# One product for each block of z and its convolution, in a two-layer graph network on one Trainium2 core

## The chip, the cores and the metric

The kernel runs on one core of one Trainium2 chip. It is one launch that computes the whole network. The metric is the device time of one execution in microseconds (us); the times given are medians of several executions. A core has five engines, each with its own in-order queue of instructions: TensorE (PE), which multiplies matrices into PSUM; VectorE (DVE); ScalarE (ACT); GpSimd (POOL); and SyncE (SP), which here only issues transfers. An instruction that waits holds everything behind it in its queue.

## What is computed

The network has 3125 nodes of 256 channels, 50,000 edges and two layers. Each layer adds to x a graph block and a mixing block, and then a feed-forward block. The change concerns the mixing block of the second layer, a hyperbolic linear attention. Cut to what matters (the sequence length is 1, so of each width-5 convolution only the centre tap acts, and `proj`, `expmap0` and `logmap0` reduce to scalings of a row by a function of its norm):

```python
h = conv1d(logmap0(proj(x, c), c), w_qkv, pad=2)       # 256 -> 768 channels
h = relu(batchnorm(h, bn_gamma, bn_beta))
t = logmap0(proj(proj(expmap0(h, c), c), c), c)
s = conv1d(t, w_dw, pad=2, groups=t.shape[1])          # one weight per channel
s = conv1d(s, w_pw, pad=0, groups=t.shape[1] // DIM)   # 24 blocks of 32 x 32
cat = concatenate([t, s], axis=1)                      # 1536 channels
t2 = logmap0(proj(proj(expmap0(cat, c), c), c), c)
q, k, v = split(t2.reshape(N, 16, 96, L), 3, axis=2)   # 16 heads of 32
vk = einsum('ngdl,ngel->ngde', v, relu(k))
out = einsum('ngde,ngdl->ngdl', vk, relu(q)) / (sum(v, -1) + ATT_EPS)
```

After it come another norm, a 512 to 256 convolution `w_res` with its bias, and a last hyperbolic scaling.

## The kernel before

The nodes lie in 25 tiles of 125 rows; four tiles form a chunk (the last chunk is one tile). The first layer, and the product that makes the 768 channels `z` of the second, run until about 1234 us. `z` is stored in DRAM in transposed form: channels on partitions, nodes in the free dimension.

Then `layer1` plans its work. Streams are written as Python generators that yield `Op(engine, cost, ...)` before each step. `Flow.run` is a planner: it picks, again and again, the step that can start earliest by the costs in the code (ties go by urgency), and the order in which the steps are picked is the order of the instructions on all engines. A step can take and give buffers by name: `z` has one buffer, `cat`, `r`, `ST` and `Sb` two, `S` and `kvg` three, and `nm` is a set of three PSUM banks that many streams share. The costs decide the order; at run time each engine follows that order and waits where a result is late.

The streams of this stage are:

- `group` and `attend`, the edge attention, 25 blocks (`b`) of 17 slots in three groups. POOL gathers rows of k and v (line 1524, `kvg`). SP loads the queries `q3` (line 1532), the one-hot matrices `ST` (line 1537) and `Sb` (line 1545). ACT widens `Sb` to `S` (line 1551). PE spreads the queries (line 1560, `qe`), DVE multiplies by k (line 1564), sums per head (line 1583, `sco`), ACT takes the exponential (line 1590), DVE weights v (line 1593), and PE sums over the edges (line 1601, `es`). `attend` then divides and multiplies by a weight matrix (`wvT` line 1619, `wp` line 1626).
- `hyper`, the mixing block, one stream per tile, two tiles sharing one `z` load (a pair, 13 in all). It is the code that changes.
- `hyper_end`, its last norms per chunk, and `mlp_stream`, the graph block's feed-forward part (`hp_g` line 703, `dn_g` line 717).
- After all edge blocks: routing, the scatter of rows (line 1980) and the expert products (lines 2083 and 2098), with the shared expert (`hp_s` line 2009, `dn_s` line 2023) beside them on PE until the end.

In `hyper`, the pair's `z` comes by one transfer on SP (line 1642) and ACT applies batch norm and relu to its six blocks of 128 channels (line 1645). The channels are arranged so that block `3 * h + m` holds four heads' groups of one kind: `m` is 0 for k, 1 for q, 2 for v, and `h` is the half. Four PSUM accumulators `cat_{t}_{i}` follow for each tile. Accumulators 0 and 1 hold three blocks each, transposed by PE (line 1662); 2 and 3 hold the convolution of three blocks each (line 1664), where `bd` holds the six 128 x 128 block-diagonal matrices of `w_pw`, scaled by `w_dw` (line 1484). ACT empties each: the first two by one copy (line 1674), the others by a relu of k (line 1676) and a copy of q and v (line 1677), and each by a square whose row sums go to `n2` (line 1679). The last product of a pair's second tile frees `z`, and the next pair's load may then start. DVE and ACT form the attention from `cat` (lines 1685 to 1715), PE transposes it (line 1720) and multiplies by `wres` (line 1727).

The tile `wxt`, which `bd` views, serves the first layer before: its columns hold the weights `wx` of the products `xm` (line 921), which end at about 88 us. Then `w_pw` is loaded into it (line 1474).

Of the kernel before, what the change touches and what calls it, by code (L numbers as in the profile page):

```python
# [7 lines left out]
F32 = mybir.dt.float32  # L8
BF16 = mybir.dt.bfloat16
I32 = mybir.dt.int32  # L10
AF = mybir.ActivationFunctionType
OP = mybir.AluOpType
AX = mybir.AxisListType
# [7 lines left out]
P = 125  # L21
# [10 lines left out]
NH, HD = 8, 32  # L32
# [118 lines left out]
def kernel(ctx: ExitStack, tc: tile.TileContext, a: dict, out: bass.AP):  # L151
    nc = tc.nc


    keep = ctx.enter_context(tc.tile_pool(name="keep", bufs=1))
# [16 lines left out]
    def nm_tile(shape, name):  # L172
        return ps_tile("nm", shape, name)
# [59 lines left out]

    wxt = keep.tile([128, 6 * 128], F32, name="wxt")
    xbt = keep.tile([128, C + 1 + 2 * NH * 4], F32, name="xbt")
# [14 lines left out]
    ident = keep.tile([128, 128], F32, name="ident")  # L250
# [19 lines left out]
    tiny = keep.tile([128, 1], F32, name="tiny")  # L270
# [128 lines left out]
    for k in range(2):  # L399
        po = nm_tile([128, 2 * NQ], f"wxqk_{k}")  # L400
# [1062 lines left out]
    def layer1(lists):  # L1463
# [8 lines left out]
        wp = lp.tile([128, 2, C], F32, name="wp")  # L1472
        bd = wxt.rearrange("p (m d) -> p m d", m=6)
        nc.sync.dma_start(out=bd, in_=a["w_pw"].rearrange("m p d -> p m d"))
# [157 lines left out]
        def hyper(t, pair, ch):  # L1632
# [18 lines left out]
            todo = []  # L1651
            for i in range(4):
                s, h = divmod(i, 2)
                last = i == 3 and t == t0 + nt - 1
                mk = yield Op("PE", 0.48 if s == 0 else 0.86, [pair["ready"]],
                              take=["nm"] + (["cat"] if i == 0 else []),
                              give=["z"] if last else [])
                po = nm_tile([P, 3, 128], f"cat_{t}_{i}")
                for m in range(3):
                    zm = pair["z"][:, 3 * h + m, at_]  # L1660
                    if s == 0:
                        nc.tensor.transpose(po[:, m, :], zm, ident)
                    else:
                        nc.tensor.matmul(po[:, m, :], zm, bd[:, 3 * h + m, :],
                                         start=True, stop=True)
                todo.append((mk, po, i))
                while len(todo) == 2 or (todo and i == 3):
                    mk, po, q = todo.pop(0)
                    full = yield Op("ACT", 1.15 if q < 2 else 1.35, [mk],
                                    give=["nm"])  # L1670
                    if q == 0:
                        cat = lp.tile([P, 4, 3, 128], F32, tag="cat", name=f"cat_{t}", bufs=2)
                    if q < 2:
                        nc.scalar.copy(cat[:, q], po)
                    else:
                        nc.scalar.activation(cat[:, q, 0, :], po[:, 0, :], AF.Relu)
                        nc.scalar.copy(cat[:, q, 1:, :], po[:, 1:, :])
                    sq = lp.tile([P, 512], BF16, tag="sq", name=f"sq_{t}_{q}")
                    nc.scalar.activation(sq[:, :384], po.rearrange("p m d -> p (m d)"), AF.Square,
                                         accum_out=pair["n2"][:, t - t0, q : q + 1])  # L1680
# [3 lines left out]
            m = yield Op("DVE", 0.68, [full])  # L1684
            nc.vector.tensor_reduce(ks, cat[:, :, 0, :].rearrange("p q (g d) -> p q g d", d=HD),
                                    AX.X, OP.add)
            s12 = ch["s12"][:, j : j + 1]
            if t == t0 + nt - 1:
                m = yield Op("DVE", 0.4, [m, full])
                nn = lp.tile([P, 2], F32, tag="nn", name=f"nn_{t}", bufs=2)[:, :nt]  # L1690
                nc.vector.tensor_reduce(nn, pair["n2"][:, :nt, :], AX.X, OP.add)
                nc.vector.tensor_scalar(nn, nn, MIN_NORM ** 2, None, op0=OP.max)
                y, m = yield from rsqrt_by_power(nn, nt, f"nn{t}", m)
                m = yield Op("DVE", 0.17, [m])
                nc.vector.tensor_scalar(ch["s12"][:, j + 1 - nt : j + 1], y, ATANH_MAXN, 1.0,
                                        op0=OP.mult, op1=OP.min)
                pair["scale"].set(m)
# [3 lines left out]
            r = lp.tile([P, 4, 128], F32, tag="r", name=f"r_{t}", bufs=2)  # L1701
            nc.scalar.activation(r, cat[:, :, 2, :], AF.Identity, bias=tiny[:P], scale=s12)
            for q in range(2):
                m = yield Op("DVE", 1.7, [m])
                nc.vector.reciprocal(r[:, 2 * q : 2 * q + 2, :], r[:, 2 * q : 2 * q + 2, :])  # L1705
            m = yield Op("DVE", 0.68, [m])
            nc.vector.scalar_tensor_tensor(r, cat[:, :, 2, :], s12, r, op0=OP.mult, op1=OP.mult)
            m = yield Op("DVE", 0.68, [m], give=["cat"])
            nc.vector.scalar_tensor_tensor(r, cat[:, :, 1, :], 0.0, r, op0=OP.max, op1=OP.mult)
            m = yield Op("DVE", 0.68, [m])  # L1710
# [15 lines left out]
            for k in range(4):  # L1726
                nc.tensor.matmul(po, oT[:, k, :], wres[:, k, :], start=(k == 0), stop=(k == 3))  # L1727
            m = yield Op("ACT", 0.4, [m, ms], take=["ft"], give=["nm"])
# [614 lines left out]
```

## Time and profile before

| | us |
|---|---|
| median of 5 runs | 2729.35 |
| lowest, highest | 2724.88, 2730.55 |
| the profiled execution | 2732.3 |
| its span in the profile | 2730.4 |
| PE busy over the span | 2496.3 (91%) |
| DVE busy | 1338.2 (49%) |
| ACT busy | 983.6 (36%) |
| POOL busy | 1189.2 (44%) |
| mean granted PE clock | 0.961 |

The instructions of `hyper` that change, in the stage from 1234 to 2072 us, count and mean duration:

| line, engine | what | count | mean ns |
|---|---|---|---|
| 1662 PE | transposes, 128 columns | 150 | 288 |
| 1664 PE | convolution products, 128 columns (two records each) | 300 | 285 |
| 1674 ACT | copy of 384 | 50 | 478 |
| 1676 ACT | relu of 128 | 50 | 288 |
| 1677 ACT | copy of 256 | 50 | 388 |
| 1679 ACT | square of 384 | 100 | 516 |
| 1679 ACT | reading its row sums | 100 | 224 |

How to read the profile: it is one execution taken by the hardware profiler. Busy time is the union of the recorded durations of an engine. The recorded end of a PE instruction is modelled, and neighbouring records of PE and of ACT overlap, so the pace of a run of instructions is read from their starts. A product of two fp32 operands leaves two records, a transpose one. "A <- B" in the waits means that an instruction of A stood idle until B was done. The chain that ended last is followed back from the last instruction, at each step to what released it or to the instruction before it on its engine; in this profile it reaches back to 1522 us. Lines are those of the kernel before.

### The profile page before, as it was taken

To read this page: it belongs to the slowest core of one execution; us is meant where nothing else is said; L and a number is where in the kernel's file an instruction comes from. 1 tells how busy PE (TensorE), PEld (TensorE's weight loads), DVE (VectorE), ACT (ScalarE), POOL (GpSimd) and SP (SyncE) were. 2 spreads that over 40 slices of the span, in tenths; PEclk is the share of its full clock that TensorE was granted. 3 is DMA by queue.
4 is the path that set the end of the run, shared out by engine and by line. 5 is a ranking of instruction groups with operands and counts; after the bars stand their busy time and mean duration, and the time that the engine had idled before them with its cause. 6 is when DMAs were issued, how large, how long until landed. Compare 5 with 4: busy or idle time off the path is not lost. (4 is left out here: it accounts for less than half of the span.)

```text
span 2730.4 us, 32036 instructions
## 1 busy us (share of the span) xinstructions
PE 2496.3 (91%) x11409; PEld 1825.1 (67%) x11409; DVE 1338.2 (49%) x3226; ACT 983.6 (36%) x2013; POOL 1189.2 (44%) x1179
## 2 busy tenths in 40 slices
PE   5888989999999999986779888998989999999998
PEld 4555666666666555565656666767767678888886
DVE  7365123353624344266888788888885201111113
ACT  4772112222323343344336444464432222222221
POOL 3002777777770000005775676656622722222220
PEclk9989999999999999997889999999999999999999
DMA  4425666576761015127776667666620245555555
GB/s 119 161 82 178 169 196 185 167 219 176 208 186 32 1 49 148 48 64 234 235 215 186 183 209 212 187 198 195 200 76 1 79 158 192 192 203 187 195 181 149
DMA packets 186996, 426.99 MB, mean 156 GB/s; under 512 B 31433, under 2 KB 116553, under 8 KB 178634
## 3 DMA queue, kind: packets, MB, share of 16 engines
q0 software_dynamic: 80688, 281.78, 34.3%
q1 hardware_dynamic: 103593, 140.99, 16.5%
q10 hardware_dynamic: 2545, 2.09, 0.3%
q8 instruction: 92, 1.51, 0.2%
q14 instruction: 78, 0.64, 0.1%
HBM read 358.95 MB, written 65.74 MB: 156 GB/s over the span
## 5 line engine op out<-in xcount | busy, mean ns | idle before, releaser
L1524 POOL DMA_INDIRECT kvg<-kvtab,el x425 | 466.0, 1096 | 232.3 <-issue 109.1
L1083 POOL DMA_INDIRECT msg<-hs,el x425 | 418.5, 985 | 322.7 <-DMA hot<-S 193.4
L1195 ACT ACTIVATE fh<-fp,bnh,bns 128x500 f32<-128x500 f32 (+1 forms) x224 | 160.7, 723 | 371.8 <-PE fp L1191 371.5
L1601 PE MATMUL es<-kvg,S 128*125 128x264 f32 x850 | 225.7, 419 | 40.9 <-DVE kvg L1593 40.4
L2071 ACT ACTIVATE rhid<-rh,rw 128x256 f32<-128x256 f32 x256 | 121.3, 474 | 342.0 <-PE rh L2083 341.3
L2083 PE MATMUL rh<-xrT,rw 128*128 128x256 f32 x1024 | 238.3, 381 | 0.0
L1206 DVE SCALAR_TENSOR_TENSOR x<-fy,f_w,x 125x256 f32<-125x256 f32 x200 | 96.2, 482 | 276.2 <-PE fy L1203 275.8
L2098 PE MATMUL ry<-rw,rhid 128*128 128x256 f32 x1024 | 231.5, 379 | 0.0
L1601 PEld LDWEIGHTS es<-kvg,S 128*125 128x125 f32 x850 | 169.7, 204 | 88.6 <-DVE kvg L1593 52.9
L1112 PEld LDWEIGHTS <-S 128*125 128x125 bf16 x1275 | 153.0, 138 | 103.1 <-issue 85.6
L1560 PE MATMUL qe<-q,ST 125*128 125x256 bf16 x1275 | 179.3, 284 | 43.7 <-DVE kvg L1564 38.4
L1112 PE MATMUL es<-msg,S 128*125 128x256 bf16 x1275 | 182.0, 276 | 34.3 <-DMA msg<-hs,el 27.4
L2098 PEld LDWEIGHTS ry<-rw,rhid 128*128 128x128 f32 x1024 | 194.6, 190 | 26.5
L2083 PEld LDWEIGHTS rh<-xrT,rw 128*128 128x128 f32 x1024 | 193.2, 191 | 25.7 <-issue 0.5
L1203 PE MATMUL fy<-f_Wo,fh 128*125 128x256 f32 x800 | 205.5, 380 | 1.2 <-DVE x L1206 0.8
L2105 DVE TENSOR_TENSOR yr<-ry,rw 128x256 f32<-128x256 f32 x64 | 27.2, 425 | 359.7 <-PE ry L2098 359.7
L1191 PE MATMUL fp<-fh,f_W 128*128 128x500 f32 (+1 forms) x448 | 186.4, 545 | 0.3 <-ACT fh L1195 0.3
L1191 PE MATMUL fp<-xT_f,f_W 128*128 128x500 f32 (+1 forms) x448 | 186.5, 544 | 0.0
L1560 PEld LDWEIGHTS <-ST 125*128 125x128 bf16 x1275 | 128.7, 101 | 85.1 <-issue 54.4
L1319 POOL TENSOR_TENSOR xn<-xn,row_bp 125x1024 f32<-125x1024 f32 (+1 forms) x7 | 13.8, 1977 | 389.1 <-DVE hx L1293 319.1
L1203 PEld LDWEIGHTS fy<-f_Wo,fh 128*125 128x125 f32 x800 | 142.1, 188 | 54.6 <-issue 33.3
L1564 DVE TENSOR_TENSOR kvg<-qe,kvg 128x512 f32<-128x512 f32 (+1 forms) x225 | 144.8, 651 | 44.1 <-DMA kvg<-kvtab,el 26.2
(425 smaller groups left out, 4214.5 us busy)
## 6 DMA issues: line engine op xcount, KB each, us to landing
db<-dlT SPq DMA_DIRECT2D x25, 544.0 KB
ST<-dlT SPq DMA_DIRECT2D x25, 544.0 KB
hot<-S SPq DMA_DIRECT2D x50, 187.5 KB
Sb<-hot SPq DMA_DIRECT2D x50, 187.5 KB
ztab<-z SPq DMA_DIRECT2D x18, 500.0 KB
z<-ztab SPq DMA_DIRECT2D x12, 750.0 KB
xs<-pad SPq DMA_DIRECT2D x1, 8224.0 KB
xr<-xs SPq DMA_DIRECT2D x32, 257.0 KB
```

The lines of the kernel that those rows point to most:

```text
L1083: nc.gpsimd.indirect_dma_start(out=msg[:, i, :], out_offset=None, in_=hs3_rows, in_offset=bass.IndirectOffsetOnAxis(ap=el[:, b, g0 + i : g ...
L1112: nc.tensor.matmul(blk["po"], S[:, i, :], msg[:, i, r * C : (r + 1) * C], start=(g0 + i == 0 and r == 0), stop=(g0 + i == LE - 1 and r == 2))
L1191: nc.tensor.matmul(ps[q][:, :n], self.ws[e][i][:, k, q * 128 : (q + 1) * 128], h[:, k, :n], start=(k == 0), stop=(k == 1))
L1195: nc.scalar.activation(nxt[:, q, :n], ps[q][:, :n], AF.Relu, bias=self.sh[i][:, 2 * e + q : 2 * e + q + 1], scale=self.sc[i][:, 2 * e + q ...
L1203: nc.tensor.matmul(po, nxt[:, k, j * P : (j + 1) * P], self.ws[e][2][:, k, :], start=(k == 0), stop=(k == 1))
L1524: nc.gpsimd.indirect_dma_start(out=kvg[:, i, : 2 * C], out_offset=None, in_=kvtab, in_offset=bass.IndirectOffsetOnAxis(ap=el[:, b, g0 + i ...
L1560: nc.tensor.matmul(pq[i0][:, i, :], ST[:P, g0 + i0 + i, :], blk["q3"][:, r, :], start=(r == 0), stop=(r == 2))
L1564: nc.vector.tensor_tensor(kvg[:, i0 : i0 + k, :C], pq[i0][:, :k, :], kvg[:, i0 : i0 + k, :C], OP.mult)
L1601: nc.tensor.matmul(blk["pa"], S[:, i, :], kvg[:, i, C:], start=(g0 + i == 0), stop=(g0 + i == LE - 1))
L2071: nc.scalar.activation(hid[-1][:, q % 2, :], ps, AF.Gelu, bias=w1[:, 8 * C + q : 8 * C + q + 1])
L2083: nc.tensor.matmul(ps, w1[:, k * 4 * C + h * 128 : k * 4 * C + (h + 1) * 128], xrT[:, k, :], start=(k == 0), stop=(k == 1))
L2098: nc.tensor.matmul(po, hid[k // 2][:, k % 2, r * 128 : (r + 1) * 128], w2[:, k * C : (k + 1) * C], start=(k == 0), stop=(k == 7))
```

## The change

`wxt` grows from six blocks of 128 columns to seven. Block 0 is filled with the identity by DVE at the beginning of `layer1`; the six convolution matrices follow it as blocks 1 to 6. A block of `z` is then multiplied once, with a right-hand side of 256 columns that takes block 0 and block `3 * h + i + 1` with a step between them, so that one product gives the transposed block and its convolution side by side. The transposes are gone.

A tile has three accumulators in place of four, one for each kind: k, q and v. Each is 512 columns: block and convolution of half 0, block and convolution of half 1. ACT empties the accumulator of k by one relu of 512 and those of q and v by one copy of 512, and each by one square of 512. `cat` is arranged by kind accordingly, so that DVE and ACT read contiguous columns later; the four sums of squares become three; and the rows of `wres` are taken in another order, since the order of the 512 attention channels is now half, then block before convolution. The planner's costs of these steps change with them: four PE steps of 0.48, 0.48, 0.86 and 0.86 us become three of 0.95, and four ACT steps of 1.15, 1.15, 1.35 and 1.35 become three of 1.4.

```diff
-    wxt = keep.tile([128, 6 * 128], F32, name="wxt")
+    wxt = keep.tile([128, 7 * 128], F32, name="wxt")
...
-        bd = wxt.rearrange("p (m d) -> p m d", m=6)
+
+        both = wxt.rearrange("p (m d) -> p m d", m=7)
+        nc.vector.tensor_copy(both[:, 0, :], ident)
+        bd = both[:, 1:, :]
         nc.sync.dma_start(out=bd, in_=a["w_pw"].rearrange("m p d -> p m d"))
...
-            for i in range(4):
-                s, h = divmod(i, 2)
-                last = i == 3 and t == t0 + nt - 1
-                mk = yield Op("PE", 0.48 if s == 0 else 0.86, [pair["ready"]],
+            for i in range(3):
+                last = i == 2 and t == t0 + nt - 1
+                mk = yield Op("PE", 0.95, [pair["ready"]],
                               take=["nm"] + (["cat"] if i == 0 else []),
                               give=["z"] if last else [])
-                po = nm_tile([P, 3, 128], f"cat_{t}_{i}")
-                for m in range(3):
-                    zm = pair["z"][:, 3 * h + m, at_]
-                    if s == 0:
-                        nc.tensor.transpose(po[:, m, :], zm, ident)
+                po = nm_tile([P, 4, 128], f"cat_{t}_{i}")
+                for h in range(2):
+                    nc.tensor.matmul(po[:, 2 * h : 2 * h + 2, :], pair["z"][:, 3 * h + i, at_],
+                                     both[:, 0 : 3 * h + i + 2 : 3 * h + i + 1, :], start=True, stop=True)
+                todo.append((mk, po, i))
+                while len(todo) == 2 or (todo and i == 2):
+                    mk, po, q = todo.pop(0)
+                    full = yield Op("ACT", 1.4, [mk], give=["nm"])
+                    if q == 0:
+                        cat = lp.tile([P, 3, 4, 128], F32, tag="cat", name=f"cat_{t}", bufs=2)
+                        nc.scalar.activation(cat[:, 0], po, AF.Relu)
                     else:
-                        nc.tensor.matmul(po[:, m, :], zm, bd[:, 3 * h + m, :],
-                                         start=True, stop=True)
-                todo.append((mk, po, i))
-                while len(todo) == 2 or (todo and i == 3):
-                    mk, po, q = todo.pop(0)
-                    full = yield Op("ACT", 1.15 if q < 2 else 1.35, [mk],
-                                    give=["nm"])
-                    if q == 0:
-                        cat = lp.tile([P, 4, 3, 128], F32, tag="cat", name=f"cat_{t}", bufs=2)
-                    if q < 2:
                         nc.scalar.copy(cat[:, q], po)
-                    else:
-                        nc.scalar.activation(cat[:, q, 0, :], po[:, 0, :], AF.Relu)
-                        nc.scalar.copy(cat[:, q, 1:, :], po[:, 1:, :])
                     sq = lp.tile([P, 512], BF16, tag="sq", name=f"sq_{t}_{q}")
-                    nc.scalar.activation(sq[:, :384], po.rearrange("p m d -> p (m d)"), AF.Square,
+                    nc.scalar.activation(sq, po.rearrange("p q d -> p (q d)"), AF.Square,
                                          accum_out=pair["n2"][:, t - t0, q : q + 1])
...
-            nc.vector.tensor_reduce(ks, cat[:, :, 0, :].rearrange("p q (g d) -> p q g d", d=HD),
+            nc.vector.tensor_reduce(ks, cat[:, 0].rearrange("p q (g d) -> p (q g) d", d=HD),
...
-                nc.vector.tensor_reduce(nn, pair["n2"][:, :nt, :], AX.X, OP.add)
+                nc.vector.tensor_reduce(nn, pair["n2"][:, :nt, :3], AX.X, OP.add)
...
-            nc.scalar.activation(r, cat[:, :, 2, :], AF.Identity, bias=tiny[:P], scale=s12)
+            nc.scalar.activation(r, cat[:, 2], AF.Identity, bias=tiny[:P], scale=s12)
...
-            nc.vector.scalar_tensor_tensor(r, cat[:, :, 2, :], s12, r, op0=OP.mult, op1=OP.mult)
+            nc.vector.scalar_tensor_tensor(r, cat[:, 2], s12, r, op0=OP.mult, op1=OP.mult)
...
-            nc.vector.scalar_tensor_tensor(r, cat[:, :, 1, :], 0.0, r, op0=OP.max, op1=OP.mult)
+            nc.vector.scalar_tensor_tensor(r, cat[:, 1], 0.0, r, op0=OP.max, op1=OP.mult)
...
-                nc.tensor.matmul(po, oT[:, k, :], wres[:, k, :], start=(k == 0), stop=(k == 3))
+                nc.tensor.matmul(po, oT[:, k, :], wres[:, 2 * (k % 2) + k // 2, :], start=(k == 0), stop=(k == 3))
```

## The prediction

> **What bounds the kernel now.** I read four views: busy time by stretch, the waits, the chain that ended last, and the timelines of TensorE (PE) and ScalarE (ACT) around the products that change.
>
> The changed products run only in the second layer's planned stage, from 1234 to about 2072 us. Busy time by stretch; the columns are stretch, length, then busy us (and instructions) of PE, PE weight loads, VectorE (DVE), ACT and GpSimd (POOL), granted PE clock, DMA share, GB/s:
>
> ```profile
> 1234.00:1521.00 287.00, 222.27 (x1182) 173.68 (x1182) 227.19 (x382) 130.02 (x330) 186.12 (x173) 0.88 0.73 224
> 1521.00:2014.00 493.00, 436.16 (x2321) 338.43 (x2321) 413.90 (x680) 238.47 (x552) 303.44 (x278) 0.95 0.62 189
> 2014.00:2072.00 58.00, 50.78 (x220) 38.77 (x218) 51.27 (x198) 19.22 (x45) 12.17 (x9) 0.91 0.07 21
> 2072.00:2215.00 143.00, 136.55 (x543) 92.65 (x542) 35.94 (x111) 33.01 (x52) 73.92 (x108) 0.98 0.27 83
> 2215.00:2730.00 515.00, 508.23 (x2383) 439.38 (x2381) 76.07 (x183) 131.17 (x275) 122.13 (x124) 0.99 0.54 181
> ```
>
> To see: over the stage's 838 us PE is busy 709 us (85%), DVE 692 (83%), ACT 388 (46%). No engine is saturated; PE and DVE share the bound through waits on each other. After 2072 us PE is busy 136.55 + 508.23 of 658 us, so whatever the stage gains or loses arrives at the end undiminished. The waits of the stage say the same (engine, line, what released it: us in total, times, longest):
>
> ```profile
> PE es L1601 <- DVE kvg L1593: 40.4, 29, 6.2
> PE qe L1560 <- DVE kvg L1564: 38.4, 30, 4.8
> DVE kvg L1564 <- DMA kvg<-kvtab,el: 26.2, 11, 9.1
> DVE kvg L1593 <- ACT kvg L1590: 15.8, 15, 4.0
> DVE xn L1628 <- PE wp L1626: 15.5, 8, 3.6
> ACT cat L1674 <- PE cat L1662: 20.0, 12, 5.6
> SPq L1642 <- PE cat L1664: 84.8, 4, 31.7
> ```
>
> The last line is the one place where the changed step holds others: the load of the next z waits in SyncE's (SP's) queue for the last product on the old z, with the edge loads behind it.
>
> **The change on PE.** What one product costs is read from a run without gaps; start, duration, work (the recorded ends overlap, so the pace is start to start):
>
> ```profile
> 1642.34 0.82 PE L1664 MATMUL cat<-wxt,z 128*125 128x128 f32 x6
> 1643.00 1.03 PE L1626 MATMUL wp<-wp,wvT 128*125 128x256 f32 x4
> 1643.86 0.82 PE L1560 MATMUL qe<-q,ST 125*128 125x256 bf16 x6
> 1644.52 0.49 PE L1662 MATMUL cat<-ident,z 128*125 128x128 f32 x3
> 1644.85 0.82 PE L1560 MATMUL qe<-q,ST 125*128 125x256 bf16 x6
> ```
>
> Three convolution products are six records and take 1643.00 - 1642.34 = 0.66 us, 0.22 each. Three transposes are three records, one each, and take 0.33 us, 0.11 each. Two products 256 wide (wp) are four records, 0.86 us, 0.43 each. A tile (125 nodes) has six transposes and six products now: 6 x 0.11 + 6 x 0.22 = 1.98 us. Afterwards it has six products of 256: 6 x 0.43 = 2.58. So PE gets 0.60 us more per tile, 25 x 0.60 = +15.0 us: the convolution half costs what it did, and the transposes lose their single pass. The weight loads fall by a third, but they ran beside the products already.
>
> How much reaches the end? All of it (+15.0), if PE bounds throughout; none, if PE's idle 15% takes it. The chain decides. It reaches back to 1522 us; adding up its pieces by line gives 8.11 us for the convolution products (line 1664, 13 pieces) and 3.31 for the transposes (line 1662, 6 pieces), 11.4 us. After 1522 us there are 90 transpose records and 180 product records, those of 15 tiles: 15 x 1.98 = 29.7 us, so 38% lies on the chain. I take 38% of 15.0 = +5.7, keeping 0 and 15.0 as ends.
>
> [...] If a transpose cost what a product costs, the sum would be 12 x 0.22 = 2.64 against 2.58, a gain of 1.5 us over 25 tiles.
>
> **The change on ACT.** One drain of the old second kind and the start of the next; start, duration, work:
>
> ```profile
> 1570.51 0.28 ACT L1676 ACTIVATE cat<-cat 125x128 f32<-125x128 f32 x1
> 1570.67 0.38 ACT L1677 COPY cat<-cat 125x256 f32<-125x256 f32 x1
> 1570.92 0.52 ACT L1679 ACTIVATE sq<-cat 125x384 bf16<-125x384 f32 x1
> 1571.30 0.23 ACT L1679 ACTIVATION_READ_ACCUMULATOR sq<-cat 125x1 f32 x1
> 1571.39 0.31 ACT L1676 ACTIVATE cat<-cat 125x128 f32<-125x128 f32 x1
> ```
>
> By durations the change saves a lot, but these overlap. By starts this drain takes 0.88 us (1571.39 - 1570.51), the old first kind, a copy of 384 in place of relu and copy, 0.36 + 0.38 + 0.10 = 0.84. A tile: 2 x 0.88 + 2 x 0.84 = 3.44 us. The pace grows by (0.36 - 0.16) / 256 = 0.78 ns a column, so a copy or relu of 512 takes 0.46, a square of 512 0.49, the accumulator 0.10: three drains of 1.05 are 3.15. ACT saves 0.29 per tile, 7.3 us. On the chain the four changed ACT operations are only 2.84 us in all; 8% of that, scaled to 838 us from 550, is -0.4. Ends: 0 and -7.3, as ACT is 46% busy.
>
> **Order.** The stage's instruction order is written by a planner from costs in the code. They change from 2.68 to 2.85 us per tile for PE and from 5.0 to 4.2 for ACT, so all five queues are reordered: in the built program the z loads move by up to two places among the edge loads on SP (z of tile 10 from within block 9's Sb loads to after them), the last block's first two Sb loads swap, and two more activation tables are loaded.
>
> ```profile
> L1590 ACT ACT_TABLE_LOAD x21 | 26.9, 1283 | 14.0 <-issue 10.7 <-DVE sco L1588 3.0
> ```
>
> Each is 1.28 us. Some lie just ahead of the exp that DVE waits for: 0 to +2.6, I take half, +1.3. In the timeline one load begins at 1551.79 and the next activation at 1553.09, 1.30 us later, so nothing more comes with it. [...] What reordering does otherwise no row can give in advance. Its size is bounded by the stalls that such an order makes now, of which one more or one less is likely: 7.29 us for the z load at 1648.00, 6.58 for an Sb load at 1571.60. I take 0, ends -7 and +7.
>
> **The rest.** The identity is copied once into the weight tile by DVE, 128 x 128: nearest row, the scaling of a weight block of that size, 0.28 us. The copy waits until the first layer's xm products (line 921) have read that tile; queued behind it on DVE are the last bias addition (line 924) and the key maximum. DVE idles 0.85 us there for those same products, so the wait is covered and the copy itself delays line 924: 0 to 0.3, I take +0.3. The w_pw load waited for these products before too and stays so. DVE's reads of cat become contiguous at the same length, output weights are only renumbered, the norm sums three columns for four: 0, within 0.1 us a tile. z becomes free after six steps per pair and not eight; that is a rival below.
>
> **Sum.** 5.7 - 0.4 + 1.3 + 0.3 = +6.9 us. The profiled execution took 2732.3 us (span 2730.4), 2.95 above the median 2729.35. 2732.3 + 6.9 = 2739.2; against the median 2729.35 + 6.9 = **2736 us**, +0.25%. Time measured within 0.2% (5.5 us) is about what this kernel's measurement can't tell from no change.
>
> **Rivals.**
> - PE bounds throughout. For it: 88% busy after 1521 us, and most DVE waits on PE are short and many. Against: 79 us of PE waits for DVE that could take it. +15.0 + 2.6 + 0.3 = +18: 2747.
> - z comes free earlier (the other side). There is one z buffer; its load takes 5 to 7 us and blocks the Sb, q3 and ST loads behind it. On the chain: the z loads 18.3 us in three pieces, an Sb load behind one 6.6, the relu of z 9.9, in all 34.8. Two steps less per pair, each queueing on PE among edge products, plus 2 x 0.29 us of ACT, could halve that: -17.4 + 5.7 = -12: 2717. It decides from a gain of about 7 us, a fifth of the 34.8. Against: the planner reckons with the earlier release and issues the next load, and what waits on it, just as much earlier.
> - The change is swallowed: the added PE time falls where PE waits for DVE and ACT's saving where ACT idles: 2729.
>
> **How the numbers follow.** The forecast has 0.40, spread from 2729 to 2743 by the order's 7 us; of that 0.16 lies under 2734.8, within 0.2%, and 0.24 above. PE-bound has 0.18, slower; z earlier 0.25, faster; swallowed 0.17, of it 0.13 within 0.2% and 0.04 faster by a luckier order. Faster 0.25 + 0.04 = 0.29, same 0.16 + 0.13 = 0.29, slower 0.24 + 0.18 = 0.42. The range reaches from the z rival's 2717 to the PE rival's 2747, widened by a little for the order and leaving out the outer part of both: 2716 to 2750. The forecast's own is 2729 to 2743.
>
> **What will show it.** Right: 300 product records of 256 columns in place of 450 of 128, at 0.43 us a product (two records), PE's issue time in the stage up by 15 us, ACT pace per drain 1.05, stage end some 6 us later, DVE busy unchanged. PE wrong: the products of 256 with a step between the two blocks run slower than wp's 0.43, or the stage ends earlier although PE works longer: then SP's wait for z will have shrunk from the 227 us that line 1642 waits in all. Wrong altogether: a large new stall in one place, from the order.

## The result, and the profile after

The changed kernel takes 2734.57 us (median of 28 runs, 2725.39 to 2743.6) where the kernel before takes 2727.76 beside it (53 runs): a ratio of 1.0028, 95% interval 1.0020 to 1.0035, or 7.6 us more (5.5 to 9.5). The prediction was 2736, slower by 6.9. The total and the sign came out; the parts did not, and the rest of this document is about that.

One profiled execution cannot show 7.6 us (the two executions have spans of 2730.4 and 2728.0, the wrong way round), so I cut the span at three events that both kernels have and compared the stretches: the first load of z on SP, the last group of `es` products on PE, and the product of the routing's totals. Between the first two lies what I call the edge section, between the last two the tail. Columns as in the prediction: stretch, length, busy us and instructions of PE, weight loads, DVE, ACT, POOL, then granted PE clock, DMA share, GB/s. The kernel before:

```profile
0.00:1234.20 1234.20, 1142.34 (x4768) 742.20 (x4768) 533.82 (x1674) 431.88 (x761) 491.38 (x488) 0.97 0.46 133
1234.20:2013.60 779.40, 657.97 (x3499) 511.77 (x3500) 640.93 (x1061) 368.28 (x882) 489.56 (x451) 0.93 0.66 202
2013.60:2115.60 102.00, 93.83 (x439) 70.74 (x439) 69.88 (x252) 31.30 (x66) 18.92 (x13) 0.95 0.04 12
2115.60:2730.40 614.80, 602.14 (x2705) 500.40 (x2703) 93.56 (x239) 152.10 (x305) 189.30 (x227) 0.99 0.51 171
```

The changed kernel:

```profile
0.00:1229.80 1229.80, 1139.95 (x4768) 742.51 (x4768) 535.44 (x1675) 431.55 (x761) 489.56 (x488) 0.97 0.46 133
1229.80:2003.00 773.20, 658.45 (x3351) 505.01 (x3352) 640.91 (x1065) 360.84 (x763) 480.88 (x453) 0.94 0.67 204
2003.00:2113.20 110.20, 96.67 (x438) 71.80 (x437) 72.40 (x248) 30.89 (x62) 18.30 (x13) 0.91 0.04 12
2113.20:2728.00 614.80, 602.19 (x2705) 500.33 (x2703) 93.91 (x239) 152.13 (x305) 189.30 (x227) 0.99 0.51 171
```

What the reader is to see: the edge section, which holds all but one of the changed products' accumulators, is 6 us shorter in this pair of profiles, not longer. The tail, where only the last of them lies, is 8.2 us longer. After that the two are equal to 0.1 us. Before the edge section the changed kernel is 4.4 us ahead.

The changed instructions do what the prediction said of each. The groups of the changed kernel (busy us, mean ns of one, idle time before them and what ended it):

```profile
L1662 PE MATMUL cat<-wxt,z 128*125 128x256 f32 x300 | 79.1, 396 | 13.7 <-ACT z L1648 12.8 <-ACT sq L1674 0.8
...
L1674 ACT ACTIVATE sq<-cat 125x512 bf16<-125x512 f32 x75 | 45.6, 608 | 0.0
...
L1672 ACT COPY cat<-cat 125x512 f32<-125x512 f32 x50 | 29.5, 590 | 10.1 <-PE cat L1662 10.0
L695 ACT ACT_TABLE_LOAD x23 | 29.5, 1283 | 0.4
L1593 ACT ACT_TABLE_LOAD x22 | 28.2, 1283 | 4.0 <-issue 3.6
```

300 records of 256 columns; 45 table loads on these two lines where there were 43. From PE's timeline of the changed kernel (start, duration, work):

```profile
1574.34 1.03 PE L1662 MATMUL cat<-wxt,z 128*125 128x256 f32 x4
1575.20 1.03 PE L1629 MATMUL wp<-wp,wvT 128*125 128x256 f32 x4
```

Two products take 0.86 us, 0.43 each, with a step between the two blocks as without one (`wp`). And from ACT's timeline:

```profile
1560.88 0.58 ACT L1670 ACTIVATE cat<-cat 125x512 f32<-125x512 f32 x1
...
1561.93 0.37 ACT L1725 COPY ft<-ft 125x256 f32<-125x256 f32 x1
```

A drain takes 1.05 us (1561.93 - 1560.88). One sign of the prediction did not come: PE's busy time in the edge section rises by 0.5 us in this pair of profiles (658.45 against 657.97) and by 4.8 in the second, not by 15. The edge products `es` and `qe`, as many as before, are busy 393.6 and 395.9 us over the whole span in the two profiles of the changed kernel, against 405.0 and 405.1 in those of the kernel before. The waits of PE in the edge section (us in total, times, longest):

```profile
PE qe L1563 <- DVE kvg L1567: 39.4, 29, 4.9
PE es L1604 <- DVE kvg L1596: 38.5, 24, 5.2
```

and those of SP's queue before the z loads:

```profile
SPq L1645 <- PE es L1604: 98.1, 4, 27.4
SPq L1645 <- PE qe L1563: 82.7, 4, 27.3
...
SPq L1645 <- PE cat L1662: 64.0, 4, 21.9
```

On these two lines PE waits for DVE as long as before (77.9 us; 78.8 before). SP's waits for z add up to 244.8 us; in the kernel before the same sum over the edge section is 248.5. (The prediction's 227 us "in all" left out one wait of 21.8, for a transpose of line 681.)

**Where the tail's 8 us are.** PE's timeline in the tail of the changed kernel (in brackets the idle time before and what ended it):

```profile
2041.95 1.14 PE L703 MATMUL hp_g<-hT_g,gw 128*128 128x125 f32 x8
2048.50 4.98 PE L703 MATMUL hp_g<-hT_g,gw 128*128 128x125 f32 x24 [5.42 <-ACT hid_g L695]
...
2056.78 1.02 PE L1818 MATMUL tr_f<-ident,xn 125*128 125x125 f32 x8
2064.13 3.70 PE L2004 MATMUL hp_s<-xT_f,pw1s 128*128 128x500 f32 x4 [6.34 <-ACT xT_f L1822]
2067.63 3.37 PE L1828 MATMUL rt<-wr_f,xT_f 128*125 128x8 f32 x16
2070.85 3.68 PE L2004 MATMUL hp_s<-xT_f,pw1s 128*128 128x500 f32 x4
2074.33 1.87 PE L1818 MATMUL tr_f<-ident,xn 125*128 125x125 f32 x8
2076.03 2.26 PE L2004 MATMUL hp_s<-xT_f,pw1s 128*128 128x500 f32 x4
2078.13 1.81 PE L1828 MATMUL rt<-wr_f,xT_f 128*125 128x8 f32 x16
```

PE idles 5.42 and 6.34 us, and after the second it works at half pace for 12 us (`rt` x16 takes 3.37 us, then 1.81). ACT's timeline shows why it idles:

```profile
2047.68 0.42 ACT L1747 ACTIVATE sq<-ft 125x256 bf16<-125x256 f32 x1 [10.03 <-DVE ft L1741]
2048.01 0.19 ACT L1747 ACTIVATION_READ_ACCUMULATOR sq<-ft 125x1 f32 x1
2048.10 0.60 ACT L695 ACTIVATE hid_g<-hp_g,pv 128x125 f32<-128x125 f32 x2
...
2063.41 0.20 ACT L1755 ACTIVATE n<-n 125x1 f32<-125x1 f32 x1 [9.53 <-DVE n L1753]
2063.52 1.03 ACT L1822 COPY xT_f<-tr_f 128x500 f32<-128x500 f32 x2
```

Two small steps of the last chunk's `hyper_end`, which nobody needs soon, stand in ACT's queue ahead of the drains that PE needs. The order puts them there; since the planner picks what can start earliest by its costs, it must have reckoned with DVE's `ft` and `n` earlier than DVE got to them. The same two waits in the kernel before, ACT and PE:

```profile
2053.69 0.42 ACT L1752 ACTIVATE sq<-ft 125x256 bf16<-125x256 f32 x1 [5.63 <-DVE ft L1746]
2065.02 0.20 ACT L1760 ACTIVATE n<-n 125x1 f32<-125x1 f32 x1 [2.66 <-DVE n L1758]
```

```profile
2054.71 2.78 PE L1833 MATMUL rt<-wr_f,xT_f 128*125 128x8 f32 x14 [3.27 <-ACT xT_f L1827]
2065.53 1.22 PE L703 MATMUL hp_g<-hT_g,gw 128*128 128x125 f32 x4 [2.41 <-ACT hid_g L695]
```

They are 5.63 and 2.66 us, with one `xT_f` copy and three `hid_g` drains behind them, and PE idles 3.27 and 2.41. All in all PE is idle for 13.5 us of the tail (110.20 - 96.67) against 8.2 (102.00 - 93.83), and busy for 2.8 us more with nearly the same work: 5.4 + 2.8 = 8.2.

### The profile page after: what moved, and what is told of

It reads as the page before. It is cut to its first block, busy times and chain, and to the rows that moved or that the text cites. A ratio compares the mean times of both kernels' runs of the same rounds, so it can differ in the third digit from the quotient of the medians.

```text
span 2728.0 us, 31620 instructions
## 1 busy us (share of the span) xinstructions
PE 2497.3 (92%) x11259; PEld 1819.7 (67%) x11259; DVE 1342.7 (49%) x3227; ACT 975.4 (36%) x1890; POOL 1178.0 (43%) x1179
## 3 DMA queue, kind: packets, MB, share of 16 engines
q1 hardware_dynamic: 103593, 140.99, 16.5%
## 4 chain that ended last, share of the span: by engine, by line
PE 61%; DVE 14%; POOL 8%; DMA 8%; issue 5%; ACT 3%; SPq 0%; POOLq 0%; DVEq 0%; ACTq 0%
PE fp L1191 10%; PE rh L2078 8%; PE ry L2093 8%; PE fy L1203 5%; POOL msg L1083 4%; PE es L1604 4%; PE es L1112 3%; DMA msg<-hs,el 3%; DVE r L1700 2%; PE qe L1563 2%; POOL xs L1975 2%; PE hp_m L703 2%; PE dn_g L717 2%; PE z L1302 2%; DMA kvg<-kvtab,el 2%
## 5 line engine op out<-in xcount | busy, mean ns | idle before, releaser
L1527 POOL DMA_INDIRECT kvg<-kvtab,el x425 | 453.9, 1068 | 243.8 <-issue 111.1
L1604 PE MATMUL es<-kvg,S 128*125 128x264 f32 x850 | 219.8, 411 | 38.8 <-DVE kvg L1596 38.5
L2066 ACT ACTIVATE rhid<-rh,rw 128x256 f32<-128x256 f32 x256 | 121.4, 474 | 342.1 <-PE rh L2078 341.3
L1563 PE MATMUL qe<-q,ST 125*128 125x256 bf16 x1275 | 173.8, 278 | 44.2 <-DVE kvg L1567 39.4
```

The source lines that it names most:

```text
L1527: nc.gpsimd.indirect_dma_start(out=kvg[:, i, : 2 * C], out_offset=None, in_=kvtab, in_offset=bass.IndirectOffsetOnAxis(ap=el[:, b, g0 + i ...
L1563: nc.tensor.matmul(pq[i0][:, i, :], ST[:P, g0 + i0 + i, :], blk["q3"][:, r, :], start=(r == 0), stop=(r == 2))
L1604: nc.tensor.matmul(blk["pa"], S[:, i, :], kvg[:, i, C:], start=(g0 + i == 0), stop=(g0 + i == LE - 1))
L2066: nc.scalar.activation(hid[-1][:, q % 2, :], ps, AF.Gelu, bias=w1[:, 8 * C + q : 8 * C + q + 1])
```

## The experiments

Theory A is the forecast: the added PE time lengthens the edge section. Theory B says that the edge section hides most of it and that the loss is the order of the tail. In the tables of stretches below, each number is one profiled execution; "time" is the ratio to the kernel before, run beside it, turned into us.

**The same two kernels again.**

> The kernel before, unchanged, for a second trace. What it settles is how far the lengths of the stretches repeat. Two theories stand: (A) the forecast's, that the added PE time lengthens the edge section, 38% of it; (B) that the edge section is no longer than before and the loss is in the tail, from the last edge product to the routing, where the new order makes ACT wait for late DVE results with PE behind it. By both: ratio 1.000 within 0.1%; edge section (first z load to last es group) 779 us within 4, tail (last es group to the totals product) 102 us within 1.

> The changed kernel, unchanged, for a second trace. Ratio to before 1.002 to 1.0035 by both theories. Theory A (added PE time in the edge section): the edge section is 780 us or more and the 773 us of the first trace was a chance; tail between 102 and 110. Theory B (order of the tail): edge section about 773 to 779, tail again 110 within 1, with the two ACT waits of 10.0 and 9.5 us and PE idle 11 to 12 us before 2065.

Measured: 1.0004 (0.9989 to 1.0019) and 1.0031 (1.0014 to 1.0048). Stretches, beside the first two profiles:

| | first z load | edge section | tail | after it |
|---|---|---|---|---|
| before, before_again | 1234.2, 1235.8 | 779.4, 776.5 | 102.0, 101.9 | 614.8, 614.6 |
| after, after_again | 1229.8, 1232.1 | 773.2, 778.8 | 110.2, 109.9 | 614.8, 614.7 |

The tail repeats to 0.3 us, so its 8.1 us belong to the kernel. The edge section moves by 3 to 6 us from one execution to the next; what the change does to it cannot be read from single profiles.

**Only the PE work, in the order of before.**

```diff
-                        nc.tensor.transpose(po[:, m, :], zm, ident)
+                        nc.tensor.matmul(po[:, m, :], zm, ident, start=True, stop=True)
```

> The kernel before with its transposes made as plain products with the identity, 128 columns, everything else and the whole order of instructions kept. It adds 150 x 0.11 = 16.5 us of PE to the stage and nothing else. Theory A: 38% of it shows, +6.3 us, ratio 1.0023. PE bounds throughout: +16.5, 1.006. Theory B says nothing of PE being free, but needs it to be nearly so: +0 to +3 us, ratio 1.000 to 1.001; tail stays 102 us.

Measured: 1.0014 (1.0000 to 1.0028), +3.8 us (0 to 7.6); edge section 775.8, tail 101.9. The 16.5 us more of PE work cost 23% of themselves (0 to 46%), and the tail is that of the kernel before.

**Only the order, without the PE work.** The changed kernel, its product of 256 taken apart into a transpose and a product of 128:

```diff
-                    nc.tensor.matmul(po[:, 2 * h : 2 * h + 2, :], pair["z"][:, 3 * h + i, at_],
-                                     both[:, 0 : 3 * h + i + 2 : 3 * h + i + 1, :], start=True, stop=True)
+                    zm = pair["z"][:, 3 * h + i, at_]
+                    nc.tensor.transpose(po[:, 2 * h, :], zm, ident)
+                    nc.tensor.matmul(po[:, 2 * h + 1, :], zm, bd[:, 3 * h + i, :], start=True, stop=True)
```

> The changed kernel with each block transposed in one pass and its convolution a product of 128 again, written into the same accumulators; ACT, DVE, POOL and SP keep the changed kernel's instructions in its order, the planner's costs too. It takes 15 us of PE out of the stage. Theory A: 5.7 us come back, ratio to before about 1.0005. Theory B: at most 2 us come back, ratio 1.002 to 1.003, tail stays 110 us.

Measured: 1.0021 (1.0003 to 1.0039), +5.7 us; edge section 776.3, tail 106.1. Without the added work the kernel is still slower than before, and the two waits of ACT are there again (10.1 and 9.0 us). The tail is 4 us shorter than that of the changed kernel for another reason: PE's second idle time is 5.63 us in place of 6.34, and after it the half pace lasts 3.8 us, not 12. So of the tail's 8.1 us the order alone gives 4.1; the other 4 came only together with the products of 256.

**ACT's two steps planned later.** Both kernels, the last chunk alone:

```diff
-                m = yield Op("DVE", 0.5, [m])
+                m = yield Op("DVE", 0.5, [m], lag=10 if c == 6 else 0.0)
```

This is the DVE step of `ft`; in the kernel before the lag is 17, and another 3 at the step of `n`.

> The changed kernel with one planner lag more: the last chunk's square of ft is planned 10 us later, so that on ACT it comes behind the eight hid_g activations and the following n behind two xT_f copies. Every queue is as in the changed kernel until the last edge group. Theory 'tail' (the change's loss is two ACT waits of 10.0 and 9.5 us in the tail, with hid_g and xT_f queued behind them, and PE idle 5.4 and 6.3 us for it, then at half pace): the stretch from the last es group to the totals product falls from 110 us to 99 to 103, the stretch before it stays 773 to 779, the time falls by 7 to 11 us from the changed kernel's 2734 to 2723 to 2727, no slower than the kernel before. Theory 'PE work' (the loss is the 15 us more of product time in the edge section, and the tail's waits only show up where PE would have waited anyway): the time stays within 3 us of the changed kernel's, 2731 to 2736.

> The kernel before with the same kind of lag: square of ft planned 17 us later, n another 3 us, for the last chunk alone, which gives the same order of ACT in the tail as the other kernel of this pair has. Theory 'tail': the kernel before has smaller waits of the same kind (5.6 and 2.7 us, PE idle 3.3 and 2.4 us), so its tail falls from 102 us to 96 to 99 and the time by 3 to 6 us, to 2721 to 2724. If the tail's length is set by something else (DVE's small operations, or the last chunk's own chain), it stays at 102 or grows by up to 3 us: 2726 to 2730.

Measured: 1.0040 (1.0027 to 1.0053), +10.9 us, tail 112.0; and 0.9999 (0.9989 to 1.0009), tail 106.7. The repair failed, and my expectation with it. PE and ACT of the first:

```profile
2059.81 0.28 PE L1828 MATMUL rt<-wr_f,xT_f 128*125 128x8 f32 x2
2077.53 3.11 PE L1828 MATMUL rt<-wr_f,xT_f 128*125 128x8 f32 x14 [17.45 <-ACT xT_f L1822]
```

```profile
2054.42 0.42 ACT L1747 ACTIVATE sq<-ft 125x256 bf16<-125x256 f32 x1 [0.48 <-DVE ft L1741]
...
2057.40 0.58 ACT L1822 COPY xT_f<-tr_f 128x500 f32<-128x500 f32 x1 [2.46 <-PE tr_f L1818]
2076.81 0.20 ACT L1755 ACTIVATE n<-n 125x1 f32<-125x1 f32 x1 [18.84 <-DVE n L1753]
```

The first wait is gone, as meant (10.03 to 0.48 us, and PE's 5.42 with it). But the square now comes later, so DVE's `n`, which needs it, was ordered behind the normalisation of further chunks, and the wait for `n` doubled (9.53 to 18.84 us) with a copy of `xT_f` still behind it. That speaks for the mechanism, since PE idles behind a step of ACT that waits for DVE, and the longer the wait the longer the tail; but a step in an in-order queue is not made harmless by moving it back while the engine it waits for is the late one. In the kernel before, the lag takes away PE's 3.27 and 2.41 us and gives one wait of 12.6 instead. The tail of its profile is 4.7 us longer; its time is not (-3.0 to +2.5 us), which I can't explain. ACT's order in the two tails is also not the same, as I had expected: here two `xT_f` copies stand ahead of `n`, in the other kernel one.

**Other orders.** The changed kernel with other planner costs, and the kernel before with costs that add up to those of the changed kernel per tile:

```diff
-                mk = yield Op("PE", 0.95, [pair["ready"]],
+                mk = yield Op("PE", 0.89, [pair["ready"]],
...
-                    full = yield Op("ACT", 1.4, [mk], give=["nm"])
+                    full = yield Op("ACT", 1.2, [mk], give=["nm"])
```

> The changed kernel's work, with 0.89 and 1.2 us for PE's and ACT's step in the planner in place of 0.95 and 1.4. ACT's order in the tail comes out as in the kernel before; the order within the edge section is a third one, neither that of before nor of after. Theory 'tail': tail 102 us (101 to 104), edge section 772 to 782, time 2724 to 2730, level with the kernel before although PE works 15 us longer. Theory 'PE work': tail 102 too, but the edge section some 6 us longer than before's 777, time 2731 to 2736.

> The kernel before, its work unchanged, with planner costs for the four steps that add up to the changed kernel's per tile (PE 4 x 0.7125, ACT 4 x 1.05). All queues are reordered within the edge section, as far as by the change; ACT's order in the tail stays as it was. It measures what an order alone does to the edge section: I expect tail 102, edge section 777 plus or minus 6, time 2720 to 2733. If the order within the edge section matters little, 2727 plus or minus 2.

Measured: 1.0018 (1.0008 to 1.0029), +4.9 us, edge section 775.1, tail 105.6; and 0.9995 (0.9986 to 1.0005), edge section 766.2, tail 107.3. In the first, ACT's two waits are back to 5.6 and 3.1 us, PE idles 10.0 us in the tail in place of 13.5, and the changed kernel loses 4.9 us (2.2 to 7.9) in place of 7.6; the intervals overlap, so this leans towards the tail's order and does not prove it. The second shows what another order does by itself: 10 to 13 us less in the edge section and 5 us more in the tail of a single profile, and nothing in the time (-3.8 to +1.4 us).

**DVE made earlier.** If DVE is the late one, what delays it? In the tail of the changed kernel, DVE and POOL:

```profile
2044.22 2.37 POOL L1836 TENSOR_TENSOR x<-x,row_b2s 125x1024 f32<-125x1024 f32 x1 [5.50 <-DVE xn L1810]
2044.31 0.15 DVE L1737 TENSOR_SCALAR s<-rpy_n 125x1 f32<-125x1 f32 x1
2044.38 2.24 DVE L1960 TENSOR_SCALAR xn<-steps_p,part 125x4 f32<-125x4 f32 x1
2046.53 0.72 DVE L1810 TENSOR_SCALAR xn<-x,mv_f,rsy_f 125x256 f32<-125x256 f32 x2
2047.18 0.47 DVE L1741 SCALAR_TENSOR_TENSOR ft<-ft,s,xbt 125x256 f32<-125x256 f32 x1
```

A DVE instruction on four columns, 0.22 us elsewhere in this tail, takes 2.24 us and ends when POOL's addition of a bias does. Up to the DVE step that gives ACT its `n` this happens four times, for some 8 us. So I moved POOL's additions into the expert stage, which leaves the order up to the tail and ACT's order in it as they were:

```diff
-            biased_[c].set((yield Op("POOL", 2.0, [normal_[c]])))
+            biased_[c].set((yield Op("POOL", 2.0, [normal_[c], stored_[2 * c + 2]])))
```

> The changed kernel, with POOL's additions of row_b2s (2.4 us each) moved out of the tail: each waits in the planner for an expert's store, so they run in the expert stage. The order up to the tail is that of the changed kernel. In the tail DVE's instructions beside such an addition take 2.0 to 2.8 us where they take 0.15 to 0.7 alone, six of them, some 12 us, and ft and n, for which ACT waits with hid_g and xT_f queued behind, come after them. Theory 'DVE late' (the tail is long because DVE gets to ft and n late, ACT's queue stands behind them, PE idles 5.4 and 6.3 us): ft comes 4 to 5 us earlier, n 6 to 9 us earlier, PE's idle time in the tail falls from 13.5 to 2 to 6 us, the tail from 110 to 97 to 103, the time to 2721 to 2728. Theory 'order of ACT alone' (the waits would be there without POOL's additions): tail 108 to 112, time 2731 to 2736.

> The kernel before with the same move of POOL's additions. Four stretched DVE instructions (9 us) leave its tail. Theory 'DVE late': PE's idle time in the tail falls from 8.2 to 2 to 4 us, the tail from 102 to 96 to 99, the time by 3 to 6 us to 2721 to 2725; the two kernels then stand within 4 us of each other. Otherwise tail 101 to 103 and the time unchanged.

These two ran, with the next one, at a time when the kernel before itself took 2914 us: the first part and the edge section were longer (848 us in the first of them, at 185 GB/s where the four profiles above have 202 to 204), for a reason that I don't know; I call it the disturbed time. So only the ratios of that time can be used, and the tail, in which hardly anything is transferred (a DMA share of 0.04; that of the kernel with doubled products, below, is 102.8 us at that time and 103.3 outside it). The tail of the changed kernel without POOL's additions:

```profile
2176.80:2273.30 96.50, 91.52 (x438) 68.88 (x437) 60.38 (x248) 30.75 (x62) 2.81 (x6) 0.96 0.04 13
```

96.5 us in place of 110.0, with the same instructions on PE in the same order: DVE's busy time fell by 12.0 us, `ft` comes 4.0 us earlier and `n` 7.9 us earlier after the last `es` group, ACT waits 6.0 and 5.1 us and PE 1.4 and 1.6. That is what theory "DVE late" asked for (97 to 103). The order decides what stands behind `ft` and `n`; how late DVE is decides how long it stands there. In the kernel before the tail fell only from 102.0 to 100.7, close to the 101 to 103 that I had expected if DVE's delay were not the cause: PE's first idle time is gone, but the second grew from 2.4 to 4.6 us. So a late DVE is shown as the cause in the changed kernel alone.

The times are 0.9961 (0.9931 to 0.9991) for the changed kernel and 1.0004 (0.9972 to 1.0037) for the other. Part of the tail's gain is given back at the end: from the totals on the two take 621.5 and 624.1 us where all others take 613.5 to 615.2. In the first of them PE is done as early as in the changed kernel, 607 us after the totals, but the last loads and stores of the output take another 14.6 us in place of 7.2. The changed kernel with that edit is thus the only version that came out faster than the kernel before, by 0.4%, but at that time alone; it was not run again under the usual conditions. Nor did the changed kernel without the edit run at that time, so these times do not show how much of the 0.4% the edit gave: against the kernel before with the edit, the tail is 4.2 us shorter, but the first part and the edge section are shorter too, by 4.6 and 7.3 us.

**The PE work scaled up.** To size the disputed term, the kernel before with each convolution product issued twice, which keeps the order and adds 300 records of 0.11 us, 33 us:

```diff
-                        nc.tensor.matmul(po[:, m, :], zm, bd[:, 3 * h + m, :],
-                                         start=True, stop=True)
+                        for _ in range(2):
+                            nc.tensor.matmul(po[:, m, :], zm, bd[:, 3 * h + m, :],
+                                             start=True, stop=True)
```

> The kernel before with every convolution product in the edge section issued twice (150 products more, 300 records of 0.11 us, 33 us more of PE work); the order of all engines stays. It scales up the disputed cost without touching the order. By the forecast's 38% of the added PE time on the chain the edge section grows by 12.5 us from 777 to 789 and the time to 2740. By the 3.8 us (0 to 7.6) that 16.5 us more cost with products in place of transposes: +8 us (0 to 15), 2728 to 2743. If PE's idle time takes all of it, as the single profiles of that run (edge section 775.8) suggest: 777 plus or minus 3, and 2727 plus or minus 3.

> The kernel before with every convolution product issued twice once more, because the first time the kernel before itself took 2914 us and not 2727, with the edge section near 855 us and not 777: there 33 us of added PE work cost all of it, 39 us (26 to 53), while 16.5 us had cost 3.8 (0 to 7.6) where the kernel before takes 2727. If the cost of PE work depends on how long the transfers leave PE waiting, the added 33 us cost less where the kernel before takes 2727: by the share measured with 16.5 us, 23% (0 to 46%), the time rises by 8 us (0 to 15) to 2728 to 2743 and the edge section from 777 to 779 to 792. By the forecast's 38%: +12.5. If added PE work costs its full length once it is large enough, as it did there: edge section 810, time 2760.

Measured: 1.0135 (1.0089 to 1.0181) against 2914 us, and, with the kernel before at 2727 us again, 1.0028 (1.0017 to 1.0039): +7.6 us (4.6 to 10.6). The edge section of the second:

```profile
1235.40:2019.30 783.90, 675.86 (x3794) 538.96 (x3795) 641.05 (x1061) 368.63 (x882) 494.26 (x452) 0.94 0.66 201
```

So 33 us more of PE work cost 23% of themselves (14 to 32%), as 16.5 us had: the forecast's 38% was too much. For the change's 15.0 us that makes an estimate of 3.5 us (2.1 to 4.8).

The profiles also show where the rest went. Against the mean of the two profiles of the kernel before, the edge section is 5.9 us longer and PE idles 12.9 us less in it (108.0 us; 121.4 and 120.4 before). The remaining 14 us are made up by PE's other records, which got shorter, at a granted clock of 0.94 for 0.93. The groups of the edge products, in the kernel before and in the second run of this one:

```profile
L1601 PE MATMUL es<-kvg,S 128*125 128x264 f32 x850 | 225.7, 419 | 40.9 <-DVE kvg L1593 40.4
L1560 PE MATMUL qe<-q,ST 125*128 125x256 bf16 x1275 | 179.3, 284 | 43.7 <-DVE kvg L1564 38.4
```

```profile
L1601 PE MATMUL es<-kvg,S 128*125 128x264 f32 x850 | 222.7, 415 | 42.1 <-DVE kvg L1593 42.1
L1560 PE MATMUL qe<-q,ST 125*128 125x256 bf16 x1275 | 175.4, 280 | 36.3 <-DVE kvg L1564 31.2
```

In the disturbed time the same work cost its full length, 39 us (26 to 53). There neither cover shows: in the edge section PE idles 181.2 us, against 178.8 in the kernel before with POOL's additions moved, and `es` and `qe` are busy 409.6 and 410.0 us. Why, is open.

## Why the prediction was right in sum and wrong in its parts

- *The PE term, +5.7.* The 15.0 us were right as a pace (0.43 a product, 300 records), but PE's busy time rose by far less. Their share on the path was wrong: 23%, measured with two sizes of added work, in place of 38%, so an estimated +3.5 us. I took the share from the chain of one execution. A piece that lies on that chain need not lengthen the end by its own growth; the added work was taken up by PE's idle time and by shorter records of its other products (12.9 and 14 of 33 us with the products doubled).
- *The stage's end 6 us later.* Wrong. The last `es` group came at 2003.0 and 2010.9 us, against 2013.6 and 2012.3. The prediction said that an earlier end would mean that SP's wait for z had shrunk; it had not (244.8 and 248.5 us).
- *The order, 0 with ends of 7.* This is the step that failed, and the tail, which it left at nothing, is the largest difference between the profiles: +8.1 us, just beyond its upper end. The order alone accounts for 4.1 of them (the kernel with transposes); the other 4 came with the new products, by a longer idle time and the half pace after it. I looked for reordering among z loads and `Sb` loads, in the stage where the products are. It acted behind that stage, where DVE is behind its plan and a small step at the head of ACT's queue holds up PE's drains (ACT waits 10.03 and 9.53 us, PE 5.42 and 6.34). The kernel before showed the same waits there (5.6 and 2.7 us), and "a large new stall in one place, from the order" stands in the prediction as what would make it wrong altogether; but I gave it no price by stretch.
- *ACT, -0.4, and table loads, +1.3.* ACT's busy time fell by 7.4 us in the edge section although two more table loads (2.6 us) lie there; the 7.3 reckoned had no loads in it. No run separates what the two cost.
- *The copy of the identity, +0.3.* It takes 0.23 us. The bias addition behind it was released by the same product as before, so it cost nothing.
- *What I had not foreseen: -3.7 us in the first layer.* The first z load is issued at 1229.7 to 1232.1 us in the five profiles with the change's layout (mean 1230.9) and at 1232.8 to 1235.8 in six without (1234.6), those of the disturbed time left out. The cause is open; see the last section.
- *The rivals.* PE bounds throughout: no, the added work costs a quarter, except in the disturbed time, where it costs all of itself. z comes free earlier: no, SP waits as long. Swallowed: nearly true of the edge section, but not of the kernel.

Put together, the parts are 8.1 (tail) + 3.5 (PE work) - 3.7 (first layer) = 7.9, against 7.6 (5.5 to 9.5) by the times. This sum is an account, not a proof. It fits the changed kernel with the planned-later step (9.9 against 10.9, 7.4 to 14.5) and with other costs (3.4 against 4.9, 2.2 to 7.9). It does not fit the kernel with transposes (4.1 - 3.7 = 0.4 against 5.7, 0.8 to 10.6), nor the kernel before with the lag or with other costs, whose tails are 5 us longer and whose times are not. What the edge section does from order to order, which single profiles can't settle within 3 to 6 us, is missing from it. So that the tail's 8.1 us reach the end in full is likely and not shown. That the prediction's 6.9 came so near is chance: it had neither the 8.1 nor the -3.7.

## What to carry to other kernels

Where an order is planned from costs, changing a cost is itself a change: cut the profile at events that both kernels share and compare the stretches, since the difference may lie far behind the edited lines. In an in-order queue, price the steps that wait for the engine that is late, by what stands behind them, and look for what makes that engine late before moving the waiting step. A share of the chain that ended last overstated what growth costs here; adding a known amount of the same work, without touching the order, measures it, for the conditions it is run under.

## What the runs showed of the hardware

*How long the half clock lasts after an idle time varies.* After PE's 6.34 us idle in the changed kernel the granted clock is 0.50 until about 2076.7, 12.6 us after PE resumed, though PE is busy for 11.87 of the first 11.90 us; the tail of the second run has the same mean clock, 0.91. After 5.63 us in the kernel with transposes it is back after 3.8 us, after 17.45 us in the one with the lag after 5.8. So the length of the idle time alone does not set it, and no run shows what does. The tails of the changed kernel and of the one with transposes, 110.0 and 106.1 us, differ by mostly that, by an estimate of mine: 12.6 - 3.8 = 8.8 us more at a clock of 0.50 in place of 1.00 are 4.4 us of lost work.

*The same sixteen records can take 5.4 or 3.7 us.* One place in the first layer differs. In the second run of the kernel before, and of the changed kernel:

```profile
185.45 5.41 PE L717 MATMUL dn_m<-mw,hid_m 128*125 128x256 f32 x16 [1.58 <-DVE x L720]
```

```profile
184.88 3.72 PE L717 MATMUL dn_m<-mw,hid_m 128*125 128x256 f32 x16 [1.21 <-DVE x L720]
```

The 16 records take 5.41 us after an idle time of 1.58 us, and 3.72 after 1.21. In the first runs of the two kernels, where they take 5.40 and 3.72 us, the mean granted clock over them is 0.68 and 1.00. Outside the disturbed time, all five profiles with the change's layout show 3.72; of the six without, four show 5.4 and two 3.72 at the same 1.56 us, so the length of the idle time does not decide it. Nor does this place explain the first layer's gain: the two that save here issue their first z load at 1234.9 and 1235.4 us, no earlier than the four others. Where the 3.7 us come from stays open.

*POOL's addition can hold a DVE instruction until it is over.* The 2.24 us of a four-column instruction above are one of six such cases in that tail (1.98 to 2.77 us a row). Not every DVE instruction is held: the addition of line 720 takes 0.41 us at 2047.58, its usual time, while POOL's next addition runs from 2047.40 to 2049.86. No run shows what sets it apart. Moving the additions away took 12.0 us of DVE's busy time out of the tail.
